# Two transfers instead of four for each slab of the left factor

## The chip, the cores and the metric

The kernel runs on one core of one Trainium2 chip. A core has TensorE (PE, matmuls, with its weight loads shown apart as PEld), VectorE (DVE), ScalarE (ACT), GpSimd (POOL), and SyncE (SP), whose queue here issues nearly all transfers between the chip's memory (DRAM) and the on-chip memory. The transfers themselves are carried by 16 DMA engines. The metric is the time of one execution in device microseconds. Before the change it is 4308.89 us, the median of 3 runs (4305.12 to 4312.75).

## What is computed

The input `x` is an image of 512 x 512 positions with 64 channels. Two layers of the same form follow one another, each with its own weights:

```python
def _L0_conv_ref(x, src_mask, norm_scale, norm_bias, Wl, bl, Wr, br, Wlg, blg, Wrg, brg, Wog, bog, ...):
    mask = (m[:, :, None] * m[:, None, :])[..., None]
    xn = _ln(x, norm_scale, norm_bias)                 # over the 64 channels of a position
    left = (xn @ Wl + bl) * mask * sigmoid(xn @ Wlg + blg)
    right = (xn @ Wr + br) * mask * sigmoid(xn @ Wrg + brg)
    out_gate = sigmoid(xn @ Wog + bog)
    out = _banded_ingoing(left, right, 4)
    out = _ln(out, out_norm_scale, out_norm_bias) * out_gate
    return out @ Wo + bo
...
x = x + _L0_conv_ref(_gn(x), ...)
x = x + _L1_conv_ref(_gn(x), ...)
```

`_gn` normalises each pair of channels over the whole image, so a layer can begin its main work only when the image's sums are known. The hidden width is 128 channels. `_banded_ingoing` mixes rows: for every hidden channel, output row i is the sum over the nine rows k = i-4 to i+4 of `left[k, i]` times `right[k, :]`. So only a band of nine diagonals of `left` is ever needed, and for one channel the mixing is a matrix product of a banded 512 x 512 matrix with `right`.

## The kernel before

**Blocks, chunks, units.** The rows are cut into 9 overlapping blocks of 64 input rows (`row_blocks`, 56 rows apart). The columns are cut so that the two halves of the image (columns j and 256 + j) lie on the two halves of the 128 partitions. A chunk (`JC`) is 64 columns of each half, so a block has 4 chunks and a layer 36. A unit is 8 columns of a chunk (`JU`), so a chunk has 8 units.

**A period.** The layer's loop (`layer`, L925) runs one period per chunk. In each period it walks through a list of steps written out by hand (`FIRST` for layer 1, `SECOND` for layer 2, L39 and L69). An entry such as `load:13` names a step and how far from the period's unit it lies. The engines' own order is exactly this order: the wrapper `InOrder` (L488, whose line L496 all ordered instructions show in the profile) keeps it. So SP's queue is a list too, and a transfer that must wait holds all transfers behind it.

**The steps that matter here.** For a unit, `load` (L514) brings the input `z` in two transfers, one for each half of the partitions. POOL and DVE normalise it in place (`scale`, `move`, `centre`, `resc`; most on POOL), TensorE transposes and projects it, and the product with its gate goes into `RO`, the `right` factor of the last two chunks. When a chunk is complete, step `band` (`mix`, L720) multiplies, slab by slab, the banded matrix with `RO`, and `copy` writes the result over `RO`. Two periods of lag later the outputs are normalised (`norm`, on POOL and ACT), gated, projected, added to the input which `fetch` (L876) brings into `XR`, and written back by `stp` (`stored`, L909): to `mid_x` in layer 1, to the output in layer 2. In layer 1 a fetch also waits until the earlier store from its buffer has landed.

**The left factor.** The band's matrices for all 128 channels and one row block are kept in `A` on chip: for each of 8 slabs of 16 channels (`HA`), a tile of 128 partitions. Both partition halves hold the same numbers, since both halves of the columns need the same matrix: one input row on each of 64 partitions, and on it for each of the slab's 8 pairs of channels 64 output rows by 2 channels (512 bytes). They come from `left_of` in DRAM, which is zero except for the band; `spread_left` (L678) writes the band's pieces there ahead of each block. `take_left` (L706) loads one slab: for each partition half e and each half k of the 8 channel pairs one transfer.

**When slabs are loaded.** All partitions' slabs are replaced once per row block. In the block's last chunk, as soon as `copy` of a slab is done, the slab is put on a list (L1102). The next `load` step takes one slab from that list and issues it on SP ahead of its own two `z` transfers (`on_load`, L977). So in one of four periods each of the eight `load` steps carries a slab's transfers too. The first block of a layer gets its slabs in the same way while the pipeline fills (L1048). The on-chip memory of a slab is free when the matmuls of `mix` that read it are done, and the transfer waits for these.

Of the kernel before, what the change touches and what calls it, by code (L numbers as in the profile page):

```python
# [20 lines left out]
WIN = 4  # L21
NEAR = 2 * WIN + 1
S = 64
# [4 lines left out]
HA = 16  # L28
# [130 lines left out]
def tile_two_banded_layers(  # L159
# [8 lines left out]
    H = layers[0]["Wl"].shape[1]  # L168
# [19 lines left out]
    span = 2 * (S + 2 * WIN)  # L188
    size = S * H // 2 * span
    left_of = dram.tile([2, size], F32, name="left_of")  # L190
# [86 lines left out]
    def strided(v: bass.AP, at: int, *dims) -> bass.AP:  # L277

        return bass.AP(tensor=v.tensor, offset=v.offset + at, ap=[list(d) for d in dims])
# [426 lines left out]
    def take_left(n: int, h: int):  # L706

        held[h] = n
        q = HA // 4
        for e in range(2):  # L710
            for k in range(2):
                en.sync.dma_start(
                    A[e * S : (e + 1) * S, h, k * q : (k + 1) * q].rearrange("p h i t -> p h (i t)"),
                    strided(
                        left_of, n % 2 * size + (h * HA // 2 + k * q) * span + 2 * WIN,
                        (H // 2 * span, S), (span, q), (1, 2 * S),
                    ),
                )

    def mix(c: int, h: int, b: str) -> tuple:  # L720

# [203 lines left out]
    def layer(src: bass.AP, dst: bass.AP, w: dict, stats: bool, then=None):  # L925
# [51 lines left out]
        def on_load(n, t, alt, b):  # L977
            if slabs:
                take_left(*slabs.pop(0))
            if t in units and t not in early:  # L980
                load(src, units[t])
# [106 lines left out]
        def on_band(n, t, alt, b):  # L1088
            if chunk(t):
                c, h = chunk(t)  # L1090
                while held.get(h) != c // per:
                    take_left(*slabs.pop(0))
                mixed[t] = mix(c, h, b)
# [141 lines left out]
    A = keep.tile([P, H // HA, HA // 2, S, 2], F32, name="A")  # L1235
# [63 lines left out]
```

## Time and profile before

| | |
|---|---|
| median of 3 runs | 4308.89 us (4305.12 to 4312.75) |
| profiled execution, its own time | 4288.38 us |
| its span, first to last instruction | 4286.6 us |
| mean granted TensorE clock | 0.965 |
| PE busy | 3756.5 us (88%) |
| DVE busy | 3657.6 us (85%) |
| POOL busy | 3620.0 us (84%) |
| ACT busy | 3181.7 us (74%) |
| bytes moved by DMA | 596.26 MB, 139 GB/s over the span |
| `A<-left_of` transfers | 576 of 128 KB |

The profile shows one execution. An instruction appears with its engine, its operation and the tiles that it writes and reads (`z<-in_x_dram` is a load of the input into `z`). Idle time is listed with what ended it, its releaser. A row with SPq is a transfer's issue on SP's queue, not its movement. The granted clock is the share of its full speed that TensorE was allowed. Four engines are busy for three quarters of the span or more, so an average says little about which of them sets the end in a given stretch; the stretches are looked at one by one below.

### The profile page before, as it was taken

How to read it: one execution, taken by the hardware profiler on the slowest of the kernel's cores; microseconds unless marked ns; L12 is line 12 of the kernel's file. 1: busy time of each engine (PE TensorE's matmuls, PEld its weight loads, DVE VectorE, ACT ScalarE, POOL GpSimd, SP SyncE). 2: the span in 40 equal slices, each digit the busy share in tenths (PEclk: the TensorE clock that was granted, in tenths of full speed). 3: DMA queues.
4: the chain of work that ended last, by engine and by line, in shares of the span. 5: the costliest groups of instructions: out<-in, count | busy, mean ns of one | idle time of the engine just before them, and what ended most of it. 6: DMA issues, size and time to landing. Idle time of an engine off the chain costs nothing.

```text
span 4286.6 us, 223301 instructions
## 1 busy us (share of the span) xinstructions
PE 3756.5 (88%) x94986; PEld 3258.3 (76%) x94986; DVE 3657.6 (85%) x9915; ACT 3181.7 (74%) x5976; POOL 3620.0 (84%) x4962
## 2 busy tenths in 40 slices
PE   0169898989899999999995798999999999999998
PEld 0058787878788888888784687878878787878786
DVE  8988787878788888888877798989889898989897
ACT  0048787878787777878773687878888888989896
POOL 2389898989898989999855698998989898989893
PEclk9989999999999999999997899999999999999999
DMA  9843545454545444545434344444454545454533
GB/s 397 318 110 102 140 118 140 114 139 118 142 113 141 122 128 122 136 121 137 129 103 110 97 137 132 136 136 135 132 139 132 141 131 146 128 147 123 157 111 101
DMA packets 695719, 596.26 MB, mean 139 GB/s; under 512 B 138310, under 2 KB 549990, under 8 KB 692420
## 3 DMA queue, kind: packets, MB, share of 16 engines
q1 hardware_dynamic: 692212, 580.43, 47.0%
q8 instruction: 748, 12.26, 1.2%
q14 instruction: 247, 2.02, 0.2%
q0 software_dynamic: 2512, 1.56, 0.1%
HBM read 436.71 MB, written 149.74 MB: 137 GB/s over the span
## 4 chain that ended last, share of the span: by engine, by line
PE 58%; DVE 12%; POOL 9%; DMA 7%; SPq 6%; issue 5%; ACT 2%; DVEq 0%; POOLq 0%; ACTq 0%
PE banks L496 44%; PE bank L496 10%; POOL z L496 6%; SPq L496 6%; POOL on L496 3%; PE acc L496 3%; DVE sti L496 2%; DMA z<-in_x_dram 2%; DVE RO L496 2%; DVE sto L496 2%; DVE gn_st L496 2%; DMA z<-mid_x 2%; DVE XR L496 1%; DVE ZH L496 1%; ACT on L496 1%
## 5 line engine op out<-in xcount | busy, mean ns | idle before, releaser
L496 POOL TENSOR_SCALAR on<-RO,rs,nm 128x128 f32<-128x128 f32 x2520 | 1117.9, 456 | 193.3 <-PE banks L496 139.9
L496 ACT ACTIVATE on<-RO,nm,rs 128x128 f32<-128x128 f32 x2088 | 971.7, 499 | 108.4 <-PE banks L496 95.1
L496 PE MATMUL banks<-pack,ZT 64*128 64x128 f32 x9216 | 987.4, 287 | 24.4 <-DVE RO L496 15.3
L496 PE MATMUL banks<-pack,zT 64*128 64x128 f32 x9216 | 945.0, 279 | 2.2 <-issue 1.3
L496 POOL TENSOR_TENSOR z<-z,ga 128x512 f32<-128x512 f32 x556 | 649.8, 1175 | 301.9 <-DMA z<-in_x_dram 135.3
L496 ACT ACTIVATE sg<-banks 128x512 f32<-128x512 f32 x1170 | 696.1, 596 | 279.9 <-PE banks L496 253.8
L496 PEld LDWEIGHTS banks<-pack,ZT 64*128 64x128 f32 x9216 | 771.5, 194 | 148.4 <-DVE RO L496 49.6
L496 DVE TENSOR_TENSOR RO<-banks,sg 128x512 f32<-128x512 f32 x1152 | 777.6, 683 | 94.8 <-ACT sg L496 72.5
L496 DVE BATCH_NORM_STATS2 sto<-RO 128x6 f32<-128x256 f32 x2304 | 847.9, 413 | 6.7 <-ACT RO L496 2.6
L496 DVE SCALAR_TENSOR_TENSOR ZH<-banks,pack,ZH 128x896 f32<-128x896 f32 (+1 forms) x576 | 668.7, 1161 | 195.5 <-PE banks L496 163.2
L496 PEld LDWEIGHTS banks<-pack,zT 64*128 64x128 f32 x9216 | 754.0, 194 | 3.9 <-ACT zT L496 2.4
L496 PEld LDWEIGHTS banks<-RO,A 64*64 64x64 f32 x36864 | 617.2, 136 | 139.0 <-DVE RO L496 43.9
L496 PE MATMUL banks<-RO,A 64*64 64x64 f32 x36864 | 693.4, 223 | 32.3 <-issue 18.8
L496 PE MATMUL bank<-pack,ZH 128*64 128x64 f32 x18432 | 666.7, 226 | 12.5 <-DVE XR L496 5.6
L496 ACT COPY RO<-banks 128x1024 f32<-128x1024 f32 x540 | 540.2, 1008 | 173.6 <-PE banks L496 162.1
L496 POOL TENSOR_TENSOR z<-z,gb 128x512 f32<-128x512 f32 x556 | 651.5, 1177 | 3.3
L496 PEld LDWEIGHTS bank<-pack,ZH 128*64 128x64 f32 x18432 | 594.0, 139 | 72.9 <-issue 31.0
L496 ACT ACTIVATE ZH<-banks 128x896 f32<-128x896 f32 (+1 forms) x576 | 531.6, 929 | 135.2 <-PE banks L496 129.4
L496 POOL TENSOR_TENSOR z<-z,rs 128x512 f32<-128x512 f32 x586 | 611.9, 1053 | 20.9 <-DVE rs L496 20.5
L496 POOL TENSOR_TENSOR z<-z,sti 128x512 f32<-128x512 f32 x586 | 617.8, 1067 | 7.7 <-DVE sti L496 7.7
L496 PE MATMUL banks<-ZT,pack 64*128 64x448 f32 (+1 forms) x2304 | 587.3, 583 | 3.4 <-issue 1.2
L496 PE MATMUL banks<-ident,on 64*128 64x64 f32 x9216 | 461.7, 230 | 125.7 <-POOL on L496 119.3
(204 smaller groups left out, 4188.7 us busy)
## 6 DMA issues: line engine op xcount, KB each, us to landing
z<-in_x_dram SPq DMA_DIRECT2D x576, 128.0 KB
A<-left_of SPq DMA_DIRECT2D x576, 128.0 KB
z<-mid_x SPq DMA_DIRECT2D x576, 128.0 KB
gn_x<-in_x_dram SPq DMA_DIRECT2D x16, 4096.0 KB
XR<-in_x_dram SPq DMA_DIRECT2D x448, 112.0 KB
mid_x<-XR SPq DMA_DIRECT2D x448, 112.0 KB
XR<-mid_x SPq DMA_DIRECT2D x448, 112.0 KB
out_dram<-XR SPq DMA_DIRECT2D x448, 112.0 KB
```

The source lines that it names most:

```text
L496: return lambda *a, **k: tc.keep_in_program_order(f(*a, **k))
```

## The change

`take_left` loads each partition half of a slab in one transfer of 64 partitions by 8 rows of 512 bytes (256 KB), instead of two transfers of 64 partitions by 4 rows of 512 bytes (128 KB). Bytes, source, destination and place in the order stay as they are. There are 9 blocks x 8 slabs x 2 layers = 144 slab loads, so 576 transfers become 288.

```diff
     def take_left(n: int, h: int):
 
         held[h] = n
-        q = HA // 4
         for e in range(2):
-            for k in range(2):
-                en.sync.dma_start(
-                    A[e * S : (e + 1) * S, h, k * q : (k + 1) * q].rearrange("p h i t -> p h (i t)"),
-                    strided(
-                        left_of, n % 2 * size + (h * HA // 2 + k * q) * span + 2 * WIN,
-                        (H // 2 * span, S), (span, q), (1, 2 * S),
-                    ),
-                )
+            en.sync.dma_start(
+                A[e * S : (e + 1) * S, h].rearrange("p h i t -> p h (i t)"),
+                strided(
+                    left_of, n % 2 * size + h * HA // 2 * span + 2 * WIN,
+                    (H // 2 * span, S), (span, HA // 2), (1, 2 * S),
+                ),
+            )
```

## The prediction

> **What bounds the kernel now.** The page's part on the chain that ended last comes first. Its first line has the shares by engine. (By line it says little: L496 is the wrapper that records every ordered operation, so tiles are read below instead of lines.)
>
> ```profile
> PE 58%; DVE 12%; POOL 9%; DMA 7%; SPq 6%; issue 5%; ACT 2%; DVEq 0%; POOLq 0%; ACTq 0%
> ```
>
> TensorE leads, but 6% of the end is SP's queue issuing transfers. The view of everything issued on SP (count, then shortest/median/longest issue in ns), with who waited for it, says for whom:
>
> ```profile
> L496 SPq DMA_DIRECT2D z<-in_x_dram x592: 246/588/1962, 166.9 to 2136.8; - x198
> ...
> L496 SPq DMA_DIRECT2D A<-left_of x576: 573/614/1848, 254.4 to 4057.6; - x192
> ...
> L496 SPq DMA_DIRECT2D left_of<-left_rows x64: 550/591/1877, 359.6 to 3984.9; - x64
> ...
>   POOL z L496: 249.8, 96
> ```
>
> POOL waited 249.8 us for loads of `z`, in 96 waits. The next question is when. The table by stretches puts periods with slab loads beside periods without. A row has the stretch, its length, busy us and instructions of PE, PEld, DVE, ACT and POOL, the granted clock, the DMA engines' share and GB/s. The first two rows are from layer 2, the second of them with slab loads; the last four are from layer 1, the middle two with slab loads.
>
> ```profile
> 2903.00:2953.00 50.00, 49.54 (x1270) 43.16 (x1266) 46.97 (x128) 44.62 (x86) 48.39 (x65) 1.00 0.42 117
> 2953.00:3015.00 62.00, 52.06 (x1270) 44.75 (x1270) 47.32 (x128) 44.26 (x86) 49.84 (x66) 0.92 0.58 161
> ...
> 607.40:659.30 51.90, 51.11 (x1378) 44.86 (x1376) 45.75 (x124) 43.21 (x80) 50.28 (x71) 1.00 0.45 119
> 659.30:721.20 61.90, 55.65 (x1382) 48.81 (x1380) 47.34 (x130) 43.34 (x80) 50.32 (x70) 0.92 0.55 146
> 721.20:778.90 57.70, 52.49 (x1378) 46.45 (x1377) 45.60 (x123) 43.10 (x80) 51.70 (x71) 0.94 0.45 128
> 778.90:831.00 52.10, 51.01 (x1382) 45.19 (x1380) 45.96 (x126) 43.37 (x80) 51.00 (x72) 1.00 0.42 108
> ```
>
> The same 1270 matmuls take 50 us in layer 2 without slabs and 62 us with them: 12.0 us lost, of which 52.06 - 49.54 = 2.5 us are matmuls made slower by the dip of the granted clock to 0.92, and the rest is TensorE standing idle. In layer 1 two periods lose 61.9 + 57.7 - 51.9 - 52.1 = 15.6 us, of which 55.65 + 52.49 - 51.11 - 51.01 = 6.0 are slow matmuls. There are nine row blocks and so eight such reloads a layer: 8 x 27.6 = 221 us are at stake, and the two first fills. SP's order of time in the layer 2 period, then POOL's, shows the mechanism (start, length, what is issued or run; in brackets the idle time ahead and what ended it):
>
> ```profile
> 2982.44 1.41 SPq L496 DMA_DIRECT2D out_dram<-XR  x2
> 2983.89 2.58 SPq L496 DMA_DIRECT2D A<-left_of  x4
> 2986.58 1.19 SPq L496 DMA_DIRECT2D z<-mid_x  x2
> 2987.81 2.58 SPq L496 DMA_DIRECT2D A<-left_of  x4
> 2990.50 1.63 SPq L496 DMA_DIRECT2D z<-mid_x  x2
> 2992.17 2.58 SPq L496 DMA_DIRECT2D A<-left_of  x4
> 2994.79 2.22 SPq L496 DMA_DIRECT2D z<-mid_x  x2
> 2997.06 2.58 SPq L496 DMA_DIRECT2D A<-left_of  x4
> 2999.68 1.25 SPq L496 DMA_DIRECT2D z<-mid_x  x2
> ```
>
> ```profile
> 2994.69 1.17 POOL L496 TENSOR_TENSOR z<-z,ga 128x512 f32<-128x512 f32 x1 [5.10 <-DMA z<-mid_x]
> 2999.46 1.15 POOL L496 TENSOR_TENSOR z<-z,ga 128x512 f32<-128x512 f32 x1 [3.60 <-DMA z<-mid_x]
> ...
> 3003.37 1.15 POOL L496 TENSOR_TENSOR z<-z,ga 128x512 f32<-128x512 f32 x1 [2.32 <-DMA z<-mid_x]
> ```
>
> SP issues with hardly a pause from 2982.44 to 3000.93; the `z` loads stand in its queue behind four slabs, and POOL is idle 5.10 + 3.60 + 2.32 = 11.0 us for them. So in this stage the wait that ends last is SP's issue time.
>
> **The change, part by part.** *Issues removed.* Each slab loses two of four transfers. Four issues fill 2.58 us: 4 x 0.614 = 2.46, and three steps between of 0.04. So one costs 0.655 us, and a slab gives back 2 x 0.655 = 1.31 us of SP, if a transfer of twice the pieces costs the same issue. The code gives the pieces: a `z` load has 64 of 2 KB (588 ns), an `A` load 256 of 512 B (614), a `left_of<-left_rows` 1024 of 72 B (591). Issue does not follow the pieces, and the new transfer with 512 lies between measured ones: I take 0.614. The bounds are 0.59 and, were it proportional, 1.23 us.
>
> *Bytes and pieces moved.* Unchanged: 512 KB a slab in 1024 pieces of 512 B. Only their arrival is denser. What the DMA engines can take is bounded from their share of busy time:
>
> ```profile
> 2986.50:2999.60 13.10, 9.54 (x182) 8.11 (x180) 10.03 (x23) 10.04 (x21) 4.39 (x7) 1.00 0.69 182
> 3001.00:3011.00 10.00, 5.30 (x48) 4.70 (x50) 2.80 (x5) 1.37 (x3) 7.68 (x13) 0.50 0.72 207
> ```
>
> The train's 13.1 us with three slabs hold 0.69 x 13.1 = 9.0 us of DMA work; with the change SP needs 13.1 - 3 x 1.31 = 9.2 us. The two meet: the DMA engines become the next bound just as SP stops being it. I therefore take 0.7 us off the train's gain for `z` landing later in a fuller queue (bounds 0, and all but 0.3 us a slab, see the rivals).
>
> *Waits.* The merged transfer waits for all matmuls that read the slab, where the first of four waited for a part of them. The load is placed after the slab's last use, so I cost it at nothing; its cover is the distance between the copy that frees a slab and the next load step, and without it the price is at most the 1.31 us by which the first of the four could have gone ahead of the third. What is queued behind the slab on SP, the `z` loads, `XR` fetches and stores, only comes earlier.
>
> *Layer 2 reload.* Four slabs lie between SP's last wait and the last late `z`: 4 x 1.31 = 5.2, less 0.7 is 4.5 us of POOL's 11.0. The slow matmuls should shrink in step: 4.5/11.0 x 2.5 = 1.0. Together 5.5, times 8 is 44 us.
>
> *Layer 1 reload.* POOL's waits there:
>
> ```profile
> 676.20 1.18 POOL L496 TENSOR_TENSOR z<-z,ga 128x512 f32<-128x512 f32 x1 [2.66 <-DMA z<-in_x_dram]
> 690.84 1.16 POOL L496 TENSOR_TENSOR z<-z,ga 128x512 f32<-128x512 f32 x1 [4.40 <-DMA z<-in_x_dram]
> 714.07 1.16 POOL L496 TENSOR_TENSOR z<-z,ga 128x512 f32<-128x512 f32 x1 [3.00 <-DMA z<-in_x_dram]
> 721.28 1.18 POOL L496 TENSOR_TENSOR z<-z,ga 128x512 f32<-128x512 f32 x1 [1.52 <-DMA z<-in_x_dram]
> 729.95 1.15 POOL L496 TENSOR_TENSOR z<-z,ga 128x512 f32<-128x512 f32 x1 [5.50 <-DMA z<-in_x_dram]
> ```
>
> They add to 17.1 us. Slabs and `z` loads alternate here with stores and fetches, and SP also waits for stores to land, which the change does not shorten. At least the one slab directly ahead of each late load comes off: 5 x 1.31 = 6.6 us; at most all eight, 10.5. I take 6.6, since SP's other waits start its lateness anew. The slow matmuls in step: 6.6/17.1 x 6.0 = 2.3. Together 8.9, times 8 is 71 us.
>
> *First fills.* POOL's waits around the first slabs of layer 2 and layer 1:
>
> ```profile
> POOL z L496 <- DMA z<-mid_x: 10.8, 1, 10.8
> ```
>
> ```profile
> POOL z L496 <- DMA z<-in_x_dram: 6.6, 2, 5.1
> ```
>
> Slabs and `z` loads alternate there too. I take the reloads' proportion, (4.5 + 6.6)/(11.0 + 17.1) = 0.40 of 17.4, or 7 us (bounds 0 and 17).
>
> *Sum.* 44 + 71 + 7 = 122 us. The profiled execution took 4288.38 us (span 4286.6), the runs 4308.89 in the median, 0.5% more; 122 off the profiled one is 4166, off the median 4187. **Forecast: 4187 us.** With layer 1 at its upper bound (10.5, and 3.7 of clock) it is 4144.
>
> [...] TensorE's wait for POOL of 1.68 us is followed by a stretch at half the granted clock:
>
> ```profile
> 716.72 0.46 PE L496 MATMUL banks<-ident,z 64*128 64x64 f32 x8 [1.68 <-POOL z L496]
> ```
>
> ```profile
> 717.30:720.60 3.30, 3.30 (x50) 2.89 (x50) 1.92 (x7) 1.01 (x2) 2.46 (x3) 0.50 0.66 185
> ```
>
> So even short waits of the kind that the change leaves behind can halve the clock, and I let the clock's share shrink only in step. [...]
>
> **The rivals.** *The clock stays up* (0.08). Waits become short enough that the whole 2.5 and 6.0 us return: 8 x (4.5 + 2.5 + 6.6 + 6.0) + 7 = 164, 4145 us. For it: the periods without slabs run at 1.00. Against: the 0.50 just quoted.
>
> *The lateness vanishes* (0.08). If SP's saved time lets it get ahead before the train starts, POOL finds every `z` there: 221 + 17 = 238 off, 4071 us. Against: in layer 2 the train begins behind a store that waits for the computed result, and still holds four slabs afterwards.
>
> *The DMA engines are the bound* (0.11). If they don't go above a share of 0.74, about what the denser stretch has, the train shrinks only to 9.0/0.74 = 12.2 us, 0.3 us a slab instead of 1.31. That is 0.3/1.31 x 122 = 28 off, 4281 us. For it: 0.72 in the second of the two rows on the DMA share. Against: the pieces there arrive no faster than SP issues them, so 0.72 is no ceiling. [...]
>
> *It doesn't do what it says* (0.06). The issue grows with the pieces to 1.23 us, SP gains nothing: 4309 us. Against: 591 ns for 1024 pieces.
>
> *Slower, by the stores' landing* (0.05). In layer 1 SP stands still until a store of `mid_x` has landed, before the fetch that reuses its buffer:
>
> ```profile
> SPq L496 <- DMA mid_x<-XR: 5.8, 4, 1.8
> ```
>
> Four waits in the first slab period, 1.8 us at most. A denser burst ahead of a store delays its landing; 512 KB at the 207 GB/s quoted are 2.5 us. The gain is eaten when each of the 8 x 4 waits grows by 122/32 = 3.8 us; two whole slabs of backlog, 5.0 us, would give 4187 + 160 = 4347 us. Against: a `z` pair stands between slab and store, and the busiest stretch leaves the engines a quarter idle.
>
> **How the numbers follow.** The forecast has 0.62, and its own range is 4120 to 4250. The range of 4115 to 4283 holds it, the clock's rival and the DMA rival, and leaves out 0.08 + 0.06 + 0.05 = 0.19. A measurement of this kernel tells about 0.2%, 8.6 us, from no change. Faster: 0.62 + 0.08 + 0.08 and nearly all of 0.11, say 0.88; same: 0.06; slower: 0.06.
>
> **What would show it.** After: `A<-left_of` x288 at 256 KB and still about 614 ns; trains with 1.3 us a slab; POOL's wait for `z` down from 249.8 to about 249.8 - 8 x (4.5 + 6.6) - 7 = 154 us; the slab periods at 56.5 us in layer 2 and 8.9 less over the two in layer 1; the DMA share in the trains above 0.85. An issue near 1.2 us, or a share that stays near 0.74 with the waits as they are, would prove it wrong.

## The result and the profile after

The changed kernel takes 4241.98 us in the median (4238.39 to 4256.32), the kernel before beside it 4310.82; the ratio is 0.9842, with a 95% interval of 0.9808 to 0.9875. The forecast was 4187 with a range of 4115 to 4283: the sign and the range were right, the gain of 69 us is 56% of the 122 forecast. One of the four runs of a kernel below, the one with `z` ahead of the slab, took 6364 us at a granted clock of 0.753 and is left out of its figures.

The view of everything issued on SP (count, then shortest/median/longest issue in ns, first and last start in us, and below who waited for it), after the change:

```profile
L496 SPq DMA_DIRECT2D z<-in_x_dram x592: 229/588/1907, 167.1 to 2092.6; - x198
L496 SPq DMA_DIRECT2D z<-mid_x x592: 215/595/1967, 2167.2 to 4095.7; - x198
...
L496 SPq DMA_DIRECT2D A<-left_of x288: 592/613/1707, 255.5 to 4006.7; - x144
...
  POOL z L496: 209.3, 90
  DVE XR L496: 58.3, 13
```

and one row of the same view before that the prediction did not show:

```profile
L496 SPq DMA_DIRECT2D z<-mid_x x592: 215/595/2077, 2211.2 to 4142.7; - x198
```

Half as many loads of `A` are issued, each for 613 ns. The first and last start of the `z` loads measure each layer. Layer 1: 2136.8 - 166.9 = 1969.9 before, 2092.6 - 167.1 = 1925.5 after, 44.4 us less. Layer 2: 1931.5 before, 1928.5 after, 3.0 us less. Between the profiled executions (4288.38 and 4239.34 us) lie 49 us and between the medians 69, since the profiled execution of before was quicker than all timed runs of that kernel. So the periods are compared one by one, each from the first band matmul of a chunk to that of the next. The eight slab periods of layer 2 add to 491.2 us before and 483.0 after, 1.0 us less a block. In layer 1 the eight slab periods, each with the period behind it, add to 949.3 and 895.8, 6.7 less a block. That is 8.2 + 53.5 = 61.7 us in the periods with slabs. All other periods are 7.9 us longer after in layer 2 and 8.3 in layer 1, where nothing was changed. By about as much the profiled execution of before was quicker than its timed runs, and in the kernel with four issues and half of the bytes below the same periods are 7.0 and 15.3 us longer than before, too.

So nearly all the gain lies in layer 1. POOL's waits for `z` agree, before (the first two lines) and after:

```profile
POOL z L496 <- DMA z<-in_x_dram: 135.3, 44, 6.7
POOL z L496 <- DMA z<-mid_x: 114.5, 52, 10.8
...
POOL z L496 <- DMA z<-mid_x: 110.2, 39, 14.2
POOL z L496 <- DMA z<-in_x_dram: 90.6, 48, 4.6
```

The table by stretches (length, then busy us and instructions of PE, PEld, DVE, ACT, POOL, granted clock, DMA share, GB/s). First layer 2, where the second and third row hold slab loads; then layer 1, where the middle two do:

```profile
2647.10:2696.00 48.90, 48.60 (x1256) 42.48 (x1256) 46.67 (x126) 44.23 (x85) 48.28 (x65) 1.00 0.43 116
2696.00:2754.60 58.60, 51.03 (x1260) 44.07 (x1256) 47.16 (x127) 44.24 (x85) 49.20 (x66) 0.94 0.74 173
...
2902.60:2965.20 62.60, 52.91 (x1258) 45.55 (x1256) 47.27 (x126) 44.55 (x85) 49.27 (x65) 0.92 0.71 165
...
601.80:653.80 52.00, 51.22 (x1378) 45.18 (x1376) 46.08 (x125) 43.50 (x81) 50.68 (x71) 1.00 0.47 120
653.80:710.60 56.80, 52.38 (x1379) 45.64 (x1379) 46.50 (x125) 43.68 (x81) 50.92 (x71) 1.00 0.75 167
710.60:764.50 53.90, 51.44 (x1376) 45.08 (x1376) 46.19 (x125) 43.03 (x81) 50.77 (x71) 1.00 0.49 130
764.50:815.40 50.90, 50.49 (x1376) 44.78 (x1376) 46.02 (x125) 43.04 (x81) 50.82 (x71) 1.00 0.45 112
```

Layer 1's two slab periods now lose 56.8 + 53.9 - 52.0 - 50.9 = 7.8 us in this block, where they lost 15.6. In layer 2 the slab period is 58.6 us in one block, the shortest of the eight, and 62.6 in the next, which is the block whose 62.0 us the prediction quotes; the mean of the eight is 60.4, before 61.4. The DMA share of these periods went from 0.55 to 0.75 and from 0.58 to 0.74, with the same bytes to move. SP's train in the shorter layer 2 block, POOL's waits for it, and the DMA engines meanwhile:

```profile
2725.05 0.76 SPq L496 DMA_DIRECT2D out_dram<-XR  x2
2725.85 1.28 SPq L496 DMA_DIRECT2D A<-left_of  x2
2727.24 1.21 SPq L496 DMA_DIRECT2D z<-mid_x  x2
2728.49 1.28 SPq L496 DMA_DIRECT2D A<-left_of  x2
2729.87 2.40 SPq L496 DMA_DIRECT2D z<-mid_x  x2
2732.32 1.28 SPq L496 DMA_DIRECT2D A<-left_of  x2
2733.64 1.27 SPq L496 DMA_DIRECT2D z<-mid_x  x2
2734.96 1.67 SPq L496 DMA_DIRECT2D A<-left_of  x2
2736.67 2.28 SPq L496 DMA_DIRECT2D z<-mid_x  x2
```

```profile
2737.19 1.17 POOL L496 TENSOR_TENSOR z<-z,ga 128x512 f32<-128x512 f32 x1 [5.08 <-DMA z<-mid_x]
2740.48 1.15 POOL L496 TENSOR_TENSOR z<-z,ga 128x512 f32<-128x512 f32 x1 [2.12 <-DMA z<-mid_x]
2743.66 1.15 POOL L496 TENSOR_TENSOR z<-z,ga 128x512 f32<-128x512 f32 x1 [1.60 <-DMA z<-mid_x]
```

```profile
2728.00:2737.00 9.00, 9.00 (x178) 8.23 (x176) 8.89 (x19) 7.94 (x17) 4.11 (x7) 1.00 1.16 229
```

The train shrank from 18.5 us to 2738.95 - 2725.05 = 13.9. But POOL got the last `z` 4.7 us after its issue had ended, where it had been 3003.37 - 3000.93 = 2.4. The DMA engines run at a share of 1.16 and 229 GB/s, against 0.69 and 182 in the train before; streams of such transfers alone, shown below, reach 1.15 to 1.17 and 210 to 222, so the engines are called full here. What SP gained, 4.6 us, was half given back by the later landing (4.7 - 2.4 = 2.3 us), and POOL's waits in this block are 8.8 us, beside 11.0 in the block of before that the prediction shows.

### The profile page after: what moved, and what is told of

Read it like the earlier page. It is cut to its first block, busy times and chain, and to the rows that moved or that the text cites. A ratio compares the mean times of both kernels' runs of the same rounds, so it can differ in the third digit from the quotient of the medians.

```text
span 4237.6 us, 222986 instructions
## 1 busy us (share of the span) xinstructions
PE 3743.1 (88%) x94986; PEld 3243.0 (77%) x94986; DVE 3661.1 (86%) x9915; ACT 3184.6 (75%) x5976; POOL 3627.8 (86%) x4962
## 4 chain that ended last, share of the span: by engine, by line
PE 64%; DVE 10%; DMA 9%; POOL 8%; issue 4%; SPq 3%; ACT 2%; DVEq 0%; POOLq 0%; ACTq 0%
PE banks L496 50%; PE bank L496 11%; POOL z L496 5%; PE acc L496 3%; SPq L496 3%; POOL on L496 3%; DMA z<-mid_x 2%; DMA z<-in_x_dram 2%; DVE gn_st L496 2%; DVE RO L496 1%; DVE sto L496 1%; DVE XR L496 1%; DVE sti L496 1%; DVE ZH L496 1%; DMA A<-left_of 1%
## 5 line engine op out<-in xcount | busy, mean ns | idle before, releaser
L496 POOL TENSOR_SCALAR on<-RO,rs,nm 128x128 f32<-128x128 f32 x2520 | 1141.3, 474 | 204.0 <-PE banks L496 144.1
L496 POOL TENSOR_TENSOR z<-z,rs 128x512 f32<-128x512 f32 x586 | 620.7, 1072 | 22.8 <-DVE rs L496 22.6
L496 DVE BATCH_NORM_STATS2 sti<-z 128x6 f32<-128x128 f32 x2344 | 502.2, 282 | 60.2 <-POOL z L496 59.3
```

What stands on the lines that cost most here:

```text
L496: return lambda *a, **k: tc.keep_in_program_order(f(*a, **k))
```

## The experiments

**Half of the bytes.** Two theories stand against each other for what is left: the DMA engines' rate, or still SP's issues. The first pair of kernels leaves each slab's number of issues as it is and halves its bytes.

```diff
-                A[e * S : (e + 1) * S, h].rearrange(...)                # 8 channel pairs
+                A[e * S : (e + 1) * S, h, lo : lo + m].rearrange(...)   # 4 of them from the second block on
```

> The changed kernel, but from the second row block on each of the two transfers of a slab brings only the first 4 of its 8 channel pairs (so half of the left factor stays that of the first block): the same two issues a slab, half of the bytes. Theory A, the DMA engines became the bound (after the change a layer 2 train of slabs runs at a DMA share near 1 and 205 to 223 GB/s): with half of the slab bytes the train's DMA work falls by a third, POOL's waits for z fall well below the changed kernel's 209 us, to about 120, layer 2's slab periods from 60.5 to about 55 us, and the time to about 4170. Theory B, SP's issuing is still the bound: the issues are the same, so the time is the changed kernel's 4242 within 10 us.

Measured: 4169.3 us, ratio 0.9678 (0.9664 to 0.9693). Its rows of the SP view:

```profile
L496 SPq DMA_DIRECT2D z<-in_x_dram x592: 246/588/2019, 167.2 to 2052.5; - x198
L496 SPq DMA_DIRECT2D z<-mid_x x592: 215/595/1882, 2127.7 to 4023.6; - x198
...
  POOL z L496: 126.3, 69
```

These are near theory A's 4170 and 120 us. With the same issues and half the bytes, layer 2 takes 1895.9 us (32.6 less than in the changed kernel), layer 1 1885.3 (40.2 less). The slab periods of layer 2 fall from 483.0 to 447.0 us, 55.9 each where theory A had 55, those of layer 1 with the periods behind them from 895.8 to 858.1, and all other periods stay within 3 us in each layer. So bytes set the time in the slab periods of the changed kernel, in both layers.

```diff
-                A[e * S : (e + 1) * S, h, k * q : (k + 1) * q].rearrange(...)  # four issues of 4 channel pairs
+                A[e * S : (e + 1) * S, h, lo : lo + m].rearrange(...)          # four issues of 2, from the second block on
```

> The kernel before, but from the second row block on each of the four transfers of a slab brings only the first 2 of its 4 channel pairs: four issues a slab, half of the bytes (half of the left factor stays that of the first block). If the kernel before was bound by SP's issuing in its slab periods, as the prediction said, halving the bytes changes it little: 4290 to 4311. If its bytes already mattered, it falls to 4270 or less.

Measured: 4301.5 us, ratio 0.9986 (0.9970 to 1.0002).

```profile
  POOL z L496: 252.4, 98
```

In the kernel before, halving the same bytes changes nothing that can be told from noise, POOL's waits included (249.8 us before). So the prediction's reading of the kernel before, SP's issues as the bound in the slab periods, is right, and the change moved the bound from SP's issues to the bytes.

**What the ceiling is.** Every load of `A` and `z` writes 64 of the 128 partitions. Streams alone, without the layers' work:

```python
def low(): ...          # T[0:64, n] <- 64 rows of 8 x 512 B, sixteen times
def turns(): ...        # T[e * 64 : (e + 1) * 64, n] <- the same, e by turns
def whole(): ...        # T[:, n] <- 128 rows of 8 x 512 B, eight times
for stream in (low, turns, turns_half, whole, half_2k, whole_2k, turns, whole):
    settle()            # VectorE reads and writes T: the streams don't overlap
    stream()
```

> Nothing of the layers is computed; streams of transfers alone, 4 MB each, in this order: sixteen of 64 partitions x 8 pieces of 512 B into the lower half of the partitions; the same to lower and upper half by turns; thirty-two of 64 x 4 pieces by turns; eight of 128 x 8 pieces; thirty-two of 64 partitions x 2 KB by turns; sixteen of 128 partitions x 2 KB; then the second and the fourth again. Theory A1 (64 partitions at a time are the ceiling): the first two at about 220 GB/s (19 us for 4.2 MB), the fourth above 300 GB/s (under 14 us); 64 x 4 pieces at about 190 by the issues. Theory A2 (the pieces are the ceiling): first, second and fourth alike, about 220 GB/s, and the sixth with its 2 KB pieces faster than the fourth.

The table by stretches of that kernel, for the second stream (64 partitions of 8 pieces by turns), the fourth (128 partitions), and the two again:

```profile
47.90:67.90 20.00, 0.00 (x0) 0.00 (x0) 1.00 1.17 210
...
93.90:109.00 15.10, 0.00 (x0) 0.00 (x0) 1.00 1.13 278
147.10:166.00 18.90, 0.00 (x0) 0.00 (x0) 1.00 1.15 222
168.20:183.10 14.90, 0.00 (x0) 0.00 (x0) 1.00 1.15 281
```

The same pieces of 512 bytes move at 210 and 222 GB/s into 64 partitions at a time and at 278 and 281 into 128, each time with the engines' share above 1.1. So the transfers that span 128 partitions had the higher ceiling, by a factor of 1.27 to 1.32: theory A1's direction, though short of its 300. With larger pieces it was higher again: the sixth stream, 128 partitions of 2 KB pieces, moves at 359 GB/s with a share of 1.01 in its middle (134 to 144 us), where the middle of the fourth (94 to 104 us) has 289 and 1.16. That was theory A2's sign. The sixth reads another tensor, and the fourth has half as many transfers as the second, each twice as large; neither is separated here. Of the others, the first stream (the lower half alone) moves at 196 GB/s with a share of 1.14; the third (half as many pieces a transfer) at 197 with 0.88 and the fifth (64 partitions of 2 KB pieces) at 203 with 0.68, both below the 1.13 to 1.17 of the full ones and with 32 issues each. Why 64 partitions at a time are slower no run shows.

> The left factor is written to DRAM twice, one copy for each partition half, so a slab is one transfer of 128 partitions (512 KB) instead of two of 64 partitions. Theory A1, the ceiling of about 220 GB/s belongs to transfers that write only 64 partitions at a time: a burst then runs above 250 GB/s, pieces of 512 B take 27 ns again instead of 42 on average, POOL's waits for z fall below 120 us and the time to 4130 to 4180, less some 10 us for zeroing twice as much at the start. Theory A2, the ceiling is that of 512-byte pieces or of the memory they come from: the burst stays near 220 GB/s, and only SP's 0.66 us a slab is won: 4230 to 4250.

```diff
-        for e in range(2):
-            en.sync.dma_start(A[e * S : (e + 1) * S, h] ..., strided(left_of, ..., (H // 2 * span, S), ...))
+        en.sync.dma_start(A[:, h] ..., strided(left_of, ..., (H // 2 * span, P), ...))
...
+        for e in range(2):          # spread_left writes the band twice
             en.sync.dma_start(strided(left_of, at + e * size, ...), of)
```

Measured: 4296.6 us, ratio 0.9971 (0.9958 to 0.9984). A train of slabs in layer 2, and one of the periods in which the band is written to DRAM (layer 1):

```profile
2766.00:2774.00 8.00, 8.00 (x158) 7.26 (x156) 7.89 (x18) 6.95 (x15) 4.13 (x7) 1.00 1.13 264
```

```profile
608.70:668.10 59.40, 56.16 (x1378) 48.67 (x1376) 45.89 (x124) 43.88 (x81) 50.47 (x71) 0.97 0.51 111
```

The train's rate rose from 229 to 264 GB/s as theory A1 said, and the periods with slabs are shorter than the changed kernel's: by 16.7 us over the eight of layer 2, and by 36.8 over those of layer 1 with the periods behind them. But the period with the doubled band writes takes 59.4 us, where the changed kernel's takes 52.0; the eight of them in layer 1 are 51.6 us longer, the periods without slabs in layer 2 together 43.9, and that eats the gain. Both expectations of the total missed, and POOL's waits for `z` stay at 213.3 us, where theory A1 had less than 120. In the period shown, TensorE is busy 56.16 us for the same matmuls, and neither the clock (0.97) nor a wait in the table explains all of it.

**Which layer.** The change in layer 1 alone:

```diff
+        stage[0] = 1 if stats else 2
...
+        parts = [(0, HA // 2)] if stage[0] == 1 else [(0, HA // 4), (HA // 4, HA // 4)]
```

> The change in layer 1 alone; layer 2 keeps its four transfers. If layer 2's slab stage is bound by the DMA engines with two issues as it nearly was by SP with four, layer 2 gains nothing from the change, and this kernel takes the changed kernel's time within 10 us, 4232 to 4255. If both layers share the gain as predicted (71 of 122 in layer 1), it would take 4260 to 4275.

Measured: 4252.9 us, ratio 0.9871 (0.9847 to 0.9895). The intervals of this and the whole change overlap: most of the gain is layer 1's, and whether layer 2 adds any the times do not settle. POOL's waits for `z` are 96.6 us in layer 1, near the 90.6 of the whole change, and 117.7 in layer 2, near the 114.5 of before. The trace also shows how far one execution may stray: layer 2 takes 4129.7 - 2181.2 = 1948.5 us in it, 17.0 more than in the kernel before, whose code it has there; this execution took 20 us more than the kernel's median.

**Where the slab stands in the queue.** If the engines' queue is the bound, the order and the spacing matter more than the count of issues.

```diff
         def on_load(n, t, alt, b):
-            if slabs:
-                take_left(*slabs.pop(0))
             if t in units and t not in early:
                 load(src, units[t])
+            if slabs:
+                take_left(*slabs.pop(0))
```

> The changed kernel, but a load step issues its own two z transfers ahead of the slab, not behind it. If the lateness is DMA work queued ahead of z, each late z loses one slab of it (512 KB at 210 GB/s, 2.5 us): in layer 2 POOL's waits of a slab period fall from some 9 by up to 2.5 us, in layer 1 by some 3, and the time by 8 x 5 = 40, to about 4200. If it is SP's issues, only 1.3 us a late load: 4220.

Measured: 4215.8 us, the median of three runs, ratio 0.9774 (0.9754 to 0.9793). It lies between the two expectations, nearer to the second.

```profile
L496 SPq DMA_DIRECT2D z<-in_x_dram x592: 229/587/1778, 167.5 to 2080.1; - x198
L496 SPq DMA_DIRECT2D z<-mid_x x592: 215/595/1901, 2154.9 to 4088.4; - x198
...
  POOL z L496: 135.1, 68
  DVE XR L496: 58.8, 16
```

POOL's waits for `z` fall by 74 us, the time only by 0.7%, some 29, and layer 2 (1933.5 us, in an execution 18 us over the median) shows nothing of it. Its slab periods are 13.5 us shorter than the changed kernel's, but the periods behind them 16.0 longer. DVE waits 58.8 us for the `XR` fetches, as in the changed kernel (58.3): those still stand behind the slabs. That this is what holds the time is not shown: in the kernel with the change in layer 1 alone these waits are 19.5 us, against 77.8 before, and its layer 2 is not shorter. Neither expectation had either; the order alone does not bring the gain.

```diff
         def on_load(n, t, alt, b):
-            if slabs:
-                take_left(*slabs.pop(0))
...
         def on_tg(n, t, alt, b):
+            if slabs:
+                take_left(*slabs.pop(0))
```

> The changed kernel, but a slab is taken from the list at the step that multiplies by the gate (eight a period, spread evenly), not at the load step. If the DMA engines' queue at the moment of the z loads is the bound, pacing the same bytes over the period takes most of the rest away: POOL's waits for z from 209 to below 130 us, time 4150 to 4190. If the mean rate in the slab period is the bound (10 MB at 210 GB/s are 48 us of a period of 50), it wins little: 4220 to 4240.

Measured: **4172.8 us**, ratio 0.9679 (0.9664 to 0.9693), the fastest kernel of the study that loads the whole left factor (the last one below lies within its interval).

```profile
L496 SPq DMA_DIRECT2D z<-in_x_dram x592: 251/588/1924, 168.0 to 2065.2; - x198
L496 SPq DMA_DIRECT2D z<-mid_x x592: 215/594/1930, 2139.7 to 4025.6; - x198
...
  POOL z L496: 83.0, 61
  DVE XR L496: 17.7, 8
```

All bytes and issues are those of the changed kernel. Layer 2 takes 1885.9 us, 42.6 less than the changed kernel, layer 1 1897.2, 28.3 less. In a slab period of layer 2 (57.2 us) the engines move 183 GB/s, where the changed kernel's two shown above have 173 and 165. So the mean rate over the period was no obstacle, and the burst in front of the `z` loads was.

The same edit on the kernel before, with its four transfers a slab:

> The kernel before with its four transfers, paced in the same way. If its loss is the burst in front of the z loads, pacing alone brings most of what pacing with two transfers does, 4170 to 4220; if SP's total issue time in the period is what counts (46 to 50 us of a period), it stays above 4270.

Measured: 4233.2 us, ratio 0.9817 (0.9803 to 0.9832), between the two expectations.

```profile
  POOL z L496: 176.7, 81
```

Merging alone gives 1.6%, pacing alone 1.8%, both 3.2%: the two gains nearly add up. Issues and bursts are two costs, and neither edit does the other's work.

```diff
-                take_left(*slabs.pop(0))       # a slab at the gate-multiply step
+                take_left(*slabs.pop(0))       # one half of a slab there,
...
+        def on_gate(n, t, alt, b):
+            if slabs:
+                take_left(*slabs.pop(0))       # and one half here
```

> The paced kernel with the two transfers of a slab taken apart: one at the gate-multiply step, one at the step that computes the output gate (eight a period each), so 256 KB go into the queue at a time instead of 512. If what is left (POOL waits 83 us for z) is z standing behind 2.5 us of slab in the DMA queues, half of the slab in front of it takes a part off: 4140 to 4165. If what is left comes from elsewhere, 4165 to 4185.

Measured: 4185.8 us, ratio 0.9722 (0.9701 to 0.9742), slower than the paced kernel and at the upper end of the second expectation.

```profile
  POOL z L496: 114.4, 70
```

Smaller portions don't help; the waits for `z` grow again, from 83.0 to 114.4 us. The second place (the step of the output gate) may fall nearer to the loads; that was not tried apart.

```diff
-            for i in range(4):
-                posts.setdefault(per * NU * n - 12 + 3 * i, []).append(partial(spread_left, n, i))
+            for i in range(8):
+                posts.setdefault(per * NU * n - 24 + 3 * i, []).append(partial(spread_left, n, i // 2, (i % 2,)))
```

> The kernel with one transfer of 128 partitions a slab, paced as the paced kernel, and with its doubled band writes to DRAM begun earlier and issued one at a time instead of two. If the wide kernel lost its gain to the doubled writes standing in one period (its third period of a block takes 59 us in layer 1, where the changed kernel's takes 54), spreading them and the slabs gives 4130 to 4180. If each write of 1024 pieces of 72 B costs the same wherever it stands, the loss stays, some 8 x 9 us over the paced kernel: 4220 to 4250.

Measured: 4175.2 us, ratio 0.9698 (0.9681 to 0.9714), and POOL's waits:

```profile
  POOL z L496: 81.8, 59
```

The wide kernel's loss is gone when the slabs are paced and the doubled writes begin earlier, one at a time, so it was not a price that each write has wherever it stands; which of the two steps did it is not separated. With the burst gone, the wider transfers win nothing over the paced kernel (4175.2 us beside 4172.8).

## Why the prediction was right, and by how much it was off

*Issue does not follow the pieces*: right. 613 ns for 512 pieces, forecast 614; two transfers fill 1.28 us, forecast 1.31.

*SP's issue is what ends last in the slab periods*: right for the kernel before, shown by the unchanged 4301.5 us with half of the bytes.

*0.7 us off a train for the fuller queue*: this is the term that was mis-sized. In the block shown, the delay of the last `z` behind its issue grew by 4.7 - 2.4 = 2.3 us, POOL's waits fell by 2.2 us instead of 4.5, and another block (62.6 us) won nothing; over all eight the slab period became 1.0 us shorter, where 5.5 was forecast. The working took the share of 0.69 as a distance to a ceiling of 1 and so 9.0 us of work. The share counts the time that packets take, and here the same bytes cost more of it when the engines are full: 0.69/182 = 0.0038 of a share for each GB/s in the train before, 1.16/229 = 0.0051 after. Read in GB/s, the train before ran at 182 and the full engines at 229, so 13.1 us could shrink to 13.1 x 182/229 = 10.4 and not to 9.2. That accounts for 1.2 of the 2.3 us; for the rest no cause was found. The sentence that 0.72 was no ceiling was right; that 1 would be the ceiling at the old packet times was wrong.

*Layer 2 reload, 44 us*: 8.2 over its eight slab periods. Its four slabs follow one another with nothing but `z` loads between; that the engines fill there first for this reason is argued, not shown. *The clock's share in step*: layer 2's slow matmuls were 51.03 - 48.60 = 2.4 us after, 2.5 before, so nothing came back.

*Layer 1 reload, 71 us*: 53.5 over its eight pairs of periods, 6.7 a block where 8.9 was forecast. POOL's waits for `z` fell by 44.7 us in the layer, 5.6 a block, where 6.6 was forecast. In the block shown, POOL waits 8.9 us for `z`, 5.8 and 3.1 in its two periods:

```profile
POOL z L496 <- DMA z<-in_x_dram: 5.8, 3, 2.4
...
POOL z L496 <- DMA z<-in_x_dram: 3.1, 1, 3.1
```

The forecast was 10.5, so in this block the queue cost less than allowed for, and the granted clock is 1.00 in both periods, better than the forecast's in-step share. That block won 7.8 us. One period without slabs stands out after the change:

```profile
1896.20:1956.20 60.00, 54.56 (x1381) 47.31 (x1379) 46.47 (x126) 43.95 (x80) 51.08 (x72) 0.94 0.45 111
```

It takes 60.0 us where 52 is usual and the same period took 53.1 before. What delays TensorE in it was not found, and stays open.

*First fills, 7 us*: no gain is to be seen. POOL's waits for `z` around the first slabs are 5.8 us in layer 1 (6.6 before) and 17.8 in layer 2 (10.8 before), in one execution each.

*The rivals.* The DMA engines as the bound had 0.11 and 4281 us. Its mechanism is what happened in layer 2, with a ceiling of 229 GB/s in place of a share of 0.74; in layer 1 the forecast's own mechanism held. The result lies between the two, at 4242. The range held it because it had been drawn to take in this rival; for layer 2 that was not the forecast's mechanism. *The clock stays up* came true in the layer 1 block shown (1.00), not in layer 2's (0.94 and 0.92). The lateness did not vanish (POOL still waits 209.3 us, forecast 154), the issue did not grow with the pieces, and the stores' landing did not eat the gain.

*What would show it.* The count, the issue time, the train of 1.3 us a slab and a share above 0.85 came as stated; the waits, layer 2's 56.5 us and layer 1's 8.9 did not.

## What to carry to other kernels

A queue's issue time and the DMA engines' rate are two ceilings that may lie close together: here a slab's four issues filled 2.58 us, and its 512 KB are 2.3 us at the 229 GB/s of the full engines. Before merging transfers, work out the train under both: issues by their measured time, bytes by the highest GB/s that the same kind of transfer has shown when full, not by the busy share of a stretch that was not full (0.69 here, where the full one had 1.16). When urgent small loads share a queue with bulk loads that have slack, spacing the bulk evenly can be worth as much as halving its issues (here 1.8% and 1.6%), and the two nearly add up (3.2%).

## What was not expected of the hardware

Transfers of the same 512-byte pieces run at 210 to 222 GB/s when each spans 64 partitions, the halves by turns, and at 278 to 281 when it spans 128, and the DMA share reads 1.13 to 1.17 in both, so a share of 1.00 was not its highest.
